# A decoder layer on one core: the second Sinkhorn group's products on GpSimd

## The chip, the core and the metric

The kernel runs on one core of a Trainium2 chip. The core has a matrix engine (TensorE, PE in the profile), a vector engine (VectorE, DVE), a scalar engine (ScalarE, ACT), GpSimd (POOL) and a queue engine (SyncE, SP) that here only issues transfers. Each engine works through its own list of instructions in a fixed order; between engines they wait for one another with semaphores. The metric is the time of one execution on the device in microseconds (us), lower is better; of several executions the median is taken.

## The reference

The input is 16 sequences of 128 tokens with 1024 features. Three layers are added to it one after the other: attention with rotary positions, an autocorrelation attention against a context, and a feed-forward layer that mixes four streams of 256 features. The change touches only the last one, and of it only the matrix that mixes the streams. Each token has a 4x4 matrix of logits, and 50 rounds of a Sinkhorn iteration turn it into one whose rows and columns sum to one:

```python
def step(carry, _):
    u, v = carry
    u = -logsumexp(Z + v[..., None, :], axis=-1)     # rows
    v = -logsumexp(Z + u[..., :, None], axis=-2)     # columns
    return ((u, v), None)
(u, v), _ = lax.scan(step, (u0, v0), None, length=50)
H_res = exp(Z + u[..., :, None] + v[..., None, :])
...
x_mixed = einsum('btij,btjc->btic', (1 - g) * I + g * H_res, x_streams)
```

## The kernel before

**The work as a whole.** The 128 tokens of a sequence lie on the 128 partitions. In a first stage (up to about 380 us) queries, keys, values and the spectra of the context are computed. Then 16 batches, one for each sequence, go through attention, autocorrelation, the logits of the streams (`logits`, L635 to L662) and the branch (`branch`, L664 to L712). Each batch is a Python generator; a heap with written-out waiting times (`T_...`, `PERIOD`, `SKS`) decides the order in which the generators record their work. A scheduler then places the recorded instructions in each engine's list, and so the lists of all engines can change where one instruction is moved.

**The Sinkhorn groups.** `ENDS = [7, 13, 16]` cuts the batches into three groups of seven, six and three. When the last batch of a group has its logits, `mixed` (L852) runs the iteration for all matrices of the group at once: one row of 128 partitions holds 7x16 = 112 numbers in the first group, 96 in the second, 48 in the third. Group 1's Sinkhorn therefore begins in mid-run and runs beside later batches; group 3's can only begin when batch 15, the last one, has its logits, and it is followed only by the closing work.

**The iteration.** `sinkhorn` (L719) makes the first round with logarithms, then seven blocks of seven rounds (`REFRESH = 7`). A block begins with the exponential `P` of the logits (L753 to L755) and ends with ACT's logarithm of the scale factors (L775) and their addition (L776); the last block ends with L778 and L779. A round has two halves, rows and columns. A half is a product `T` (L766 or L768), a sum of four (`s`, L770) and a reciprocal (`r`, L771), each needing the one before; the first half of a block has no product. So a group has 7 x 13 = 91 products, on an engine that a table picks:

```python
r = sk.tile([128, 2, n, 4], FP, name=f"r{gi % 2}", bufs=2)      # L759
for d in range(2):
    T = K
    if d or it:
        T = sk.tile([128, n, 4, 4], FP, name=f"T{gi % 2}", bufs=2)
        e = POOL if SKPS[gi] & (1 << d) else DVE                 # L764
        if d:
            e.tensor_mul(flat(T), flat(K), over(...r[:, 0]..., 4))   # L766
        else:
            e.tensor_mul(T, K, of_cols(ab[:, 1]))                # L768
    s = sk.tile([128, n, 4], FP, name=f"s{gi % 2}", bufs=2)
    DVE.tensor_reduce(s, turned(T) if d else T, AX.X, ALU.add)   # L770
    DVE.reciprocal(r[:, d], s)                                   # L771
```

`SKPS = [3, 0, 0, ...]` puts both halves' products of group 1 on GpSimd, and those of groups 2 and 3 on VectorE. Sums and reciprocals are on VectorE for all groups.

**What follows a group.** `mixed` scales the matrices (L858), lays them out for TensorE (`relaid`: L818 on DVE, L825 on PE, L829 on DVE), makes one token matrix for each batch (`token_matrix`, L833: on GpSimd for groups 1 and 2, on both engines for group 3) and multiplies (`mix`, L843 on PE). For groups 1 and 2 ACT copies the result (L885) and GpSimd issues a transfer that adds it to the output (L886); for group 3 VectorE adds it (L888) and SP or ACT issues the write (L889). GpSimd also computes two products for each cross-correlation (L574 and L575) and issues a transfer for each branch (L710).

Of the kernel before, what the change touches and what calls it, by code (L numbers as in the profile page):

```python
# [47 lines left out]
PRODS, T_PRE = [1,1,1], 15.0  # L48
T_FILL, T_SPEC = 37.36, 24.48
REUSE, LNA = 'tile', 11  # L50
SKPS = [3, 0, 0, 0, 0, 0]
BIG = 3.0e38
NEG = -1.0e30

# [58 lines left out]
def tile_decoder(ctx: ExitStack, tc, x, cx, wqkv, wo, wlog, base, gate, wb, mats, toks, zero, eye4, out):  # L113
# [605 lines left out]
    def sinkhorn(Z, n, gi):  # L719
# [32 lines left out]
        for block in range((ITERS - 1) // REFRESH):  # L752
# [5 lines left out]
            for it in range(REFRESH):  # L758
# [7 lines that stand above are left out]
# [245 lines left out]
```

## Time and profile before

| what | value |
|---|---|
| executions | 1218.52, 1213.81 and 1218.15 us, median 1218.15 |
| the profiled execution | 1218.14 us, span 1216.4 us, mean granted TensorE clock 0.932 |
| busy in the span | PE 1028.5, DVE 832.5, ACT 601.4, POOL 615.5 us |
| group 1's Sinkhorn | logits 739.0 (L856), closing product 1084.4 (L818) |
| group 2's Sinkhorn | logits 995.7, closing product 1166.3 |
| group 3's Sinkhorn | logits 1097.7, closing product 1200.1 |
| ACT's logarithms that end group 2's blocks (L775) | 1052.3, 1085.4, 1107.2, 1121.8, 1136.3, 1150.9 |
| the same of group 3's blocks | 1117.0, 1131.6, 1146.2, 1160.8, 1176.2, 1188.0 |

The times of the last rows are starts in us from the beginning of the span, read from the timeline. The span is that of the instructions; the execution's own time is 1.7 us longer. A busy share is a mean over stages that have different limits: TensorE is full for the first 1000 us and almost idle from 1108 on. What a change to a late stage is worth has to be read from that stage's own rows.

### The profile page before, as it was taken

What the parts mean: (1) busy time and instruction counts of PE and PEld (TensorE: products, weight loads), DVE (VectorE), ACT (ScalarE), POOL (GpSimd) and SP (SyncE); (2) the same over time, 40 slices, a digit from 0 to 9 for tenths busy, and PEclk for the clock granted to TensorE, in tenths of its full rate; (3) what the DMA queues carried; (4) which work ended last, traced back from release to release, by engine and by line L of the source; (5) the groups of instructions that cost most, each with busy time, mean ns of one, the idle gap of its engine ahead of it and who ended that gap; (6) DMA issues with size and microseconds to landing.
All of it is one profiled execution on the core that took longest, in us unless ns stands there. A gap on an engine that the chain in (4) does not pass through costs nothing.

```text
span 1216.4 us, 17264 instructions
## 1 busy us (share of the span) xinstructions
PE 1028.5 (85%) x5048; PEld 704.1 (58%) x5048; DVE 832.5 (68%) x2853; ACT 601.4 (49%) x1333; POOL 615.5 (51%) x655
## 2 busy tenths in 40 slices
PE   4999988989997989999999999899999987574043
PEld 2888756867874566566655665565556554243042
DVE  5454133223223478778877888898889989989986
ACT  3332222123332356676767767766776686553020
POOL 1444122313354256756685667667866876563040
PEclk9999999998997999999999999999999998788566
DMA  6764468277769247867776676666765647929135
GB/s 208 233 205 124 136 196 260 80 235 225 221 200 285 77 99 171 226 166 190 182 194 189 169 190 184 177 168 178 192 168 146 185 125 230 225 87 207 18 49 107
DMA packets 129246, 209.98 MB, mean 173 GB/s; under 512 B 12288, under 2 KB 76672, under 8 KB 129152
## 3 DMA queue, kind: packets, MB, share of 16 engines
q1 hardware_dynamic: 116416, 189.24, 55.0%
q0 software_dynamic: 9168, 15.21, 8.0%
q10 hardware_dynamic: 3568, 4.43, 1.2%
q8 instruction: 40, 0.66, 0.2%
q14 instruction: 54, 0.44, 0.1%
HBM read 130.78 MB, written 77.59 MB: 171 GB/s over the span
## 4 chain that ended last, share of the span: by engine, by line
PE 55%; DVE 23%; ACT 8%; DMA 7%; POOL 3%; issue 3%; SPq 1%; DVEq 0%; ACTq 0%; POOLq 0%
PE mm L341 5%; PE mm L342 5%; PE mm L343 5%; PE ps L564 5%; PE o L555 4%; PE o L556 3%; PE o L557 3%; DVE s L770 3%; DVE r L771 3%; PE ps L319 3%; PE sc L486 3%; DMA xt<-in_x 3%; PE sm L526 2%; PE sc L483 2%; ACT pt L516 2%
## 5 line engine op out<-in xcount | busy, mean ns | idle before, releaser
L574 POOL TENSOR_TENSOR s<-s,sv 128x512 f32<-128x512 f32 x96 | 123.6, 1290 | 55.4 <-ACT s L571 52.6
L575 POOL TENSOR_TENSOR P<-P,s 128x512 f32<-128x512 f32 x96 | 122.7, 1280 | 14.6 <-DVE P L573 12.0
L351 POOL TENSOR_TENSOR ra<-ra,rb 128x512 f32<-128x512 f32 x40 | 51.6, 1311 | 142.9 <-DVE rb L350 142.9
L555 PE MATMUL o<-pw,ch 128*128 128x512 f32 x256 | 108.0, 422 | 2.1 <-DVE xt L548 1.7
L517 POOL TENSOR_SCALAR_AFFINE_SELECT pt<-pt 128x512 f32<-128x512 f32 x128 | 83.9, 672 | 50.9 <-ACT pt L516 50.4
L556 PE MATMUL o<-pw,cl 128*128 128x512 f32 x256 | 105.0, 410 | 0.4 <-POOL cl L542 0.4
L557 PE MATMUL o<-pw,ch 128*128 128x512 f32 x256 | 101.1, 395 | 0.0
L486 PE MATMUL sc<-e,e 96*128 96x128 f32 x512 | 92.9, 310 | 0.8 <-DMA e<-qd 0.8
L493 DVE TENSOR_REDUCE mx<-sc 128x4 f32<-128x512 f32 x128 | 86.2, 677 | 7.8 <-PE sc L486 7.5
L486 PEld LDWEIGHTS sc<-e,e 96*128 96x128 f32 x512 | 78.0, 194 | 16.9 <-issue 12.5
L512 PE MATMUL sc<-e,e 98*128 98x512 f32 x128 | 65.8, 546 | 23.4 <-ACT pt L516 11.9
L573 DVE TENSOR_TENSOR P<-sv,ps 128x512 f32<-128x512 f32 x96 | 64.8, 675 | 24.7 <-ACT s L571 23.3
L320 ACT COPY F<-ps 128x512 f32<-128x512 f32 x64 | 35.9, 587 | 91.7 <-PE ps L319 45.2
L348 DVE TENSOR_TENSOR ra<-mm,am 128x512 f32<-128x512 f32 x40 | 26.1, 684 | 78.4 <-PE mm L343 64.8
L564 PE MATMUL ps<-wT,e 128*128 128x512 f32 x128 | 72.4, 656 | 7.5 <-DVE P L573 3.0
L771 DVE RECIPROCAL r<-s 128x28 f32<-128x28 f32 (+2 forms) x294 | 76.2, 272 | 2.5
L516 ACT ACTIVATE pt<-sc 128x512 f32<-128x512 f32 x128 | 72.7, 596 | 10.4 <-PE sc L512 8.6
L770 DVE TENSOR_REDUCE s<-T 128x28 f32<-128x112 f32 (+2 forms) x273 | 67.7, 260 | 14.6 <-POOL T L766 7.8
L319 PE MATMUL ps<-raw,am 128*128 128x512 f32 x128 | 67.8, 636 | 10.3 <-ACT F L320 10.0
L570 ACT COPY s<-ps 64x512 f32<-64x512 f32 x96 | 56.0, 583 | 38.2 <-PE ps L564 34.1
L825 PE MATMUL ps<-pt,spread 128*128 128x112 f32 (+2 forms) x24 | 5.7, 402 | 70.9 <-DVE s L770 52.2
L512 PEld LDWEIGHTS sc<-e,e 98*128 98x128 f32 x128 | 24.7, 200 | 61.9 <-ACT pt L516 30.7
(217 smaller groups left out, 2950.7 us busy)
## 6 DMA issues: line engine op xcount, KB each, us to landing
sv<-se SPq DMA_DIRECT2D x128, 256.0 KB
xt<-in_x SPq DMA_DIRECT2D x32, 512.0 KB
e<-qd SPq DMA_DIRECT2D x32, 512.0 KB
sv<-so SPq DMA_DIRECT2D x64, 256.0 KB
raw<-in_cx SPq DMA_DIRECT2D x16, 512.0 KB
so<-F SPq DMA_DIRECT2D x16, 512.0 KB
qd<-hi SPq DMA_DIRECT2D x32, 256.0 KB
qd<-lo SPq DMA_DIRECT2D x32, 256.0 KB
```

The source lines that it names most:

```text
L319: PE.matmul(ps, lhsT=A[m], rhs=cb[:, cols], start=True, stop=True)
L486: PE.matmul(sc[:, j, :], lhsT=qs[0:96, h * 128 : (h + 1) * 128], rhs=ks[0:96, g * 128 : (g + 1) * 128], start=False, stop=j == 3,)
L512: PE.matmul(st, lhsT=ks[:, g * 128 : (g + 1) * 128], rhs=qs[:, s * 512 : (s + 1) * 512], start=True, stop=True)
L516: ACT.activation(pt.rearrange("p j t -> p (j t)"), st, AF.Exp, scale=scale)
L555: PE.matmul(ps, lhsT=h, rhs=woh[k][:, cols], start=k == 0, stop=False)
L556: PE.matmul(ps, lhsT=r, rhs=woh[k][:, cols], start=False, stop=False)
L557: PE.matmul(ps, lhsT=h, rhs=wol[k][:, cols], start=False, stop=k == NK - 1)
L564: PE.matmul(ps, lhsT=M[m], rhs=of, start=True, stop=True)
L574: POOL.tensor_mul(s, s, v[:, 1, :])
L575: POOL.tensor_add(P, P, s)
L770: DVE.tensor_reduce(s, turned(T) if d else T, AX.X, ALU.add)
L771: DVE.reciprocal(r[:, d], s)
```

## The change

One entry of the table changes, and with it the engine of 91 instructions, the products L766 and L768 of group 2 with 128x96 numbers each. The arithmetic is the same.

```diff
-SKPS = [3, 0, 0, 0, 0, 0]
+SKPS = [3, 3, 0, 0, 0, 0]
```

Since the scheduler places all instructions anew, the order on VectorE and GpSimd also changes around the moved ones. Up to group 2's first product (at 1016 us in the profile) all the lists stand as they stood.

## The prediction

> **What bounds the kernel now.** I read the busy time by stretch first, because the page's shares are means over stages. Columns: stretch, then busy us and instruction count of PE, weight load, DVE, ACT and POOL, granted clock, DMA share, GB/s.
>
> ```profile
> 1015.00:1098.00 83.00, 54.07 (x206) 30.50 (x204) 77.84 (x325) 44.47 (x106) 50.10 (x59) 0.81 0.67 183
> 1098.00:1108.00 10.00, 5.02 (x16) 3.91 (x17) 9.32 (x53) 4.26 (x16) 0.39 (x1) 0.66 1.12 233
> 1108.00:1166.00 58.00, 6.73 (x32) 5.58 (x30) 57.35 (x352) 8.79 (x24) 6.91 (x6) 0.60 0.40 69
> 1166.00:1200.00 34.00, 14.71 (x56) 12.17 (x56) 28.33 (x124) 7.55 (x16) 13.69 (x12) 0.70 0.62 93
> 1200.00:1216.40 16.40, 9.85 (x32) 8.07 (x32) 6.89 (x11) 0.00 (x0) 1.54 (x1) 0.71 0.29 96
> ```
>
> All the moved products lie behind 1015 us. From there to 1166 us DVE is busy 94, 93 and 99% of the time, with groups 2 and 3 alone on it from 1108 on. So DVE looks like the bound. The timeline shows how they share it:
>
> ```profile
> 1143.21 0.26 DVE L768 TENSOR_TENSOR T<-P,r 128x96 f32<-128x96 f32 x1
> 1143.38 0.20 DVE L766 TENSOR_TENSOR T<-P,r 128x48 f32<-128x48 f32 x1
> 1143.50 0.39 DVE L770 TENSOR_REDUCE s<-T 128x24 f32<-128x96 f32 x2
> 1143.81 0.38 DVE L771 RECIPROCAL r<-s 128x24 f32<-128x24 f32 x2
> 1144.14 0.26 DVE L766 TENSOR_TENSOR T<-P,r 128x96 f32<-128x96 f32 x1
> ...
> 1145.13 0.26 DVE L768 TENSOR_TENSOR T<-P,r 128x96 f32<-128x96 f32 x1
> ...
> 1178.03 0.21 DVE L766 TENSOR_TENSOR T<-P,r 128x48 f32<-128x48 f32 x1
> 1178.27 0.23 DVE L770 TENSOR_REDUCE s<-T 128x12 f32<-128x48 f32 x1
> 1178.54 0.23 DVE L771 RECIPROCAL r<-s 128x12 f32<-128x12 f32 x1
> 1178.80 0.21 DVE L768 TENSOR_TENSOR T<-P,r 128x48 f32<-128x48 f32 x1
> ```
>
> Two halves of group 2 take 1145.13 - 1143.21 = 1.92 us, 0.96 each, and in that time group 3 makes a half too. Alone, a half of group 3 takes 1178.80 - 1178.03 = 0.77 us. So each chain fills the other's waits: group 2 costs group 3 only 0.19 us a half. By ACT's logarithms a block takes 14.55 us shared (1121.8 to 1136.3) and 11.8 us alone (1176.2 to 1188.0). These are latency chains rather than sums of work, and what counts is the round trip of a half.
>
> That round trip on POOL shows in group 1, where POOL and DVE happened to be free:
>
> ```profile
> 780.76 0.33 DVE L771 RECIPROCAL r<-s 128x28 f32<-128x28 f32 x1
> 781.24 0.39 POOL L768 TENSOR_TENSOR T<-P,r 128x112 f32<-128x112 f32 x1 [0.31 <-DVE r L771]
> 781.65 0.27 DVE L770 TENSOR_REDUCE s<-T 128x28 f32<-128x112 f32 x1 [0.57 <-POOL T L768]
> ```
>
> The reciprocal ends at 781.09 and POOL starts at 781.24: 0.15 us for the hand-over. The product takes 0.39, and DVE goes on 0.03 after its end.
>
> **The change part by part.** 91 products leave DVE (248 ns median) for POOL. Nothing else is added, but a DVE sum now waits for POOL, and every DVE instruction behind it in the list waits with it.
>
> *The product on POOL.* The trace has no 128x96 product there. It has 128x112 (median 384 ns) and 128x512 (L575, 1280 ns), so 896 ns for 400 numbers, 2.24 ns each: 384 - 16 x 2.24 = 348 ns. Bounds: 248 (as on DVE) and 384.
>
> *A half of group 2.* Sum, start to start of the reciprocal, 0.32 (0.25 or 0.32 long in turn, and 0.03 behind); reciprocal 0.30; hand-over 0.15; product 0.35; hand-back 0.03: 1.15 us. Group 3's three instructions take some 0.37 us of DVE in each such half, so either of group 2's meets one with a chance of a third and waits some 0.06: 0.03 more. I take 1.18 us, 0.22 more than before. Bounds 1.03 (product at 248 ns, hand-over as hidden as now) and 1.30 (a product of group 3, which also reads two buffers, meets POOL's). For that last case the row is
>
> ```profile
> 1094.02 1.31 POOL L833 TENSOR_TENSOR pt<-hs,e 128x512 f32<-128x512 f32 x1
> ...
> 1094.18 1.27 DVE L766 TENSOR_TENSOR T<-P,r 128x96 f32<-128x96 f32 x1
> ```
>
> where a 0.25 us product on DVE ends only 0.12 us behind POOL's. In the new list group 3's product often stands just ahead of group 2's sum, where POOL is at work.
>
> The Trainium skill, GPSIMD Engine Reference, section "Performance versus the Vector engine", speaks against the change: it has an elementwise two-input operation on GpSimd at 1.96 times VectorE's time, and names ordinary arithmetic as VectorE's work. The rows above give 1.4 times for this small size. By the page's ratio the product would be an estimated 486 ns, the half 0.14 us longer, and the 65 halves of five blocks 9 us longer, some 1231 us in the end; the row is nearer. Its section "Specifications" has the two engines share buffer interfaces when DVE reads two inputs, which the pair of rows at 1094 us agrees with.
>
> *A block of group 2.* 13 halves with a product, 15.3; the first half without, 0.75; from the last reciprocal over ACT's logarithm, three DVE steps and the exponential to the next sum, 1.6 (1107.0 to 1108.6): 17.7 us instead of 14.55.
>
> *Part 1, up to group 3's start (1097.7).* In the new lists 26 products (two blocks) lie ahead of it; the third block, of which half stood there, follows behind. What the 26 took on DVE, and how often DVE stood idle for group 1's products, as the model for the new wait (queries by source line and by tile):
>
> ```profile
> 1015.00:1086.00 71.00, 6.14 (x14) 4.64 (x11) 0.81 0.72 199
> 1015.00:1086.00 71.00, 5.49 (x12) 4.55 (x10) 0.81 0.72 199
> ...
>   POOL T L766: 7.8, 9
>   POOL T L768: 4.8, 6
> ```
>
> (L766 above, L768 below; the figures after the length are DVE's and POOL's.) Gone: 11.6 us. New waits: 12.6 us for 91, so 0.14 x 26 = 3.6. Group 1's 21 products on POOL in this stretch now each stand behind one of group 2's; waited out every time that is 21 x 0.35 = 7.4 us, and at POOL's busy share of 0.6 (50.1 of 83 us) 4.5. Sum: -11.6 + 3.6 + 4.5 = -3.5 us for group 1's end at 1084.4, and group 3's start follows that at the old distance. Before, the layout copy L829 (1086.9) to group 3's start took 10.8 us. In the new lists block 2's last two products stand on POOL behind six token products (L833, 6.1 us from 1087.3), one more (1.05) and a transfer (L886, 1.6), and DVE's row for batch 15's logits stands behind the reciprocal that needs them: 0.35 + 6.1 + 0.35 + 1.05 + 1.6 + 0.35 + 0.6 + 0.5 = 10.9. So nothing of that chain can be gained. Bounds: -11.6 (no wait at all) and +7 (rival A).
>
> *Part 2, from group 3's start to its last product.* Before: 1200.1 - 1097.7 = 102.4 us. In the new lists group 2 then still has five blocks, and group 3 ends block six just when group 2 ends. Five blocks are 88.5. In the first of these five, POOL also issues a branch's transfer and five of group 1's (0.9 and 5 x 1.3 = 7.4 us), each between two products; POOL's free 0.8 us of each half takes in 6 x 0.8 = 4.8 at best, but each issue waits for ACT first, so 4.4 of it stays (bounds 2.6 and 7.4). Then group 3's last block alone, 11.8, with group 2's closing steps between, 1.6. Sum 106.3: +3.9 us. So what group 3 gains per half it loses to the slower group 2, which runs beside it for longer: it was alone for 34 us and will be for 13.
>
> *Part 3, the end.* Group 2's closing work holds PE from its L818 (1166.3) to the last L843 (1183.2): 17 us. It had 34 us before group 3's came; now it has 13.4, and PE's list is in order. Group 3's L825 follows its L818 by 0.5, so it waits 17 - 13.4 - 0.5 = 3.1 us. GpSimd issues the last of group 2's six transfers near that time too, and group 3's last L833 stands behind them. Bounds 0 and 6.
>
> Costed at nothing: the 91 x 0.35 = 32 us of POOL, idle 33 of 83 us from 1015 to 1098 and 51 of 58 from 1108 on; ACT and the DMAs, which only follow; the 65 x 0.25 us that leave DVE behind 1098, since the chains and not DVE's work set the pace there.
>
> Sum: -3.5 + 3.9 + 3.1 = +3.5 us on the execution's own 1218.14 (span 1216.4), which stands at the median (1218.15): 1221.7, say 1222 us.
>
> **The rivals.**
> *A, slower: POOL's queue holds both chains before group 3's start.* Groups 1 and 2 alternate on POOL behind 1.28 us products (L574, L575) that wait for ACT and for transfers. For it: group 1's blocks, with products there, took 42 to 62 us (logarithms at 790.8, 852.3, 894.6, 945.6, 989.0, 1040.8). Against it: they ran beside more work, and POOL was still idle four tenths of 1015 to 1098. Group 2's first two blocks took 70.6 us together (1014.8 to 1085.4). From 81 us on group 3 starts no earlier than at present (2 us behind them) and the result is past 0.5%; at 44 us each it starts +7 (1014.8 + 88 + 2 against 1097.7) and the time is 1218.1 + 7 + 3.9 + 3.1 = 1232.
>
> *B, slower: the tail is more costly.* A half at 1.24 (product of group 3 caught behind POOL's) adds 65 x 0.06 = 4 us: 1226; at 1.30, 1229.5. It passes 0.5% from 1.22 us a half on.
>
> *C, faster: the round trip is hidden.* With a half at 0.96 as now, part 2 loses 65 x 0.22 = 14.3 us: 1207; at 1.03, 1212. It would need DVE's hand-overs to overlap with POOL's, which the rows at 781 us, where nothing else ran, speak against.
>
> **How the numbers follow.** 0.5% is 6.1 us, about what a measurement here tells from no change: 1212.1 to 1224.2. My forecast, a small loss within it, 0.47. A 0.22 and B 0.17 are slower; C 0.10 is faster, and 0.04 for small gains in part 1 that stay within. Same 0.51, slower 0.39, faster 0.10. The forecast's own range is 1216 to 1224. The range for 8 in 10 reaches to A's 1232 and a little past it, and to the upper end of C: 1211 to 1234.
>
> **What would show it.** Group 2's blocks in the tail at 17 to 18 us by ACT's logarithms (C: under 15.5; B: over 18.2); group 3 starting near 1094 (A: 1100 or later); group 2's L818 some 13 us ahead of group 3's, not 34; products on POOL near 0.35 us; PE's L825 of group 3 behind group 2's last L843. What would make it wrong is above all the place of the waits between 1016 and 1098, where both lists are full.

## The result and the profile after

The changed kernel takes 1226.00 us (median of 15 executions, 1221.06 to 1239.50). The kernel before, run in the same comparison, takes 1214.03 (15 executions, 1210.08 to 1220.21; the three shown earlier are its first). The ratio is 1.0089, with a 95% interval of 1.0070 to 1.0108: slower by some 10.8 us, and by more than the 0.5% that can be told from no change. One execution of the changed kernel (1239.50) ran in a slower state and is left out of the ratio but not of the median, and the two medians as they stand differ by 12.0 us.

The profiled execution of the changed kernel took 1223.47 us, with a span of 1221.7 and a mean granted clock of 0.927. That is only 5.3 us above the profile of before, but the two must not be compared from their beginnings. Group 2's logits, up to which the lists of both kernels are the same, come at 995.7 us in the profile before and at 991.3 after, and in the profiles of this study between 991.3 and 1004.4. So I count from there. Z (L856) is a group's scaled logits, with which its Sinkhorn begins. The four stretches are group 2's Z to group 3's Z, on to group 3's L818, on to the end of the last L888, and on to the end of the span:

| kernel | Z to Z | to L818 | to last L888 | to the end | sum | group 2's lead at L818 |
|---|---|---|---|---|---|---|
| before | 102.0 | 102.4 | 12.2 | 4.1 | 220.7 | 33.8 |
| changed | 101.4 | 106.4 | 11.4 | 11.2 | 230.4 | 13.4 |
| difference | -0.6 | +4.0 | -0.8 | +7.1 | +9.7 | |

The sum, +9.7 us, agrees with the 10.8 us of the timed executions. The -0.6 us of the first stretch lie within the spread: in four kernels further down that differ from the kernel before only behind group 3's Z, this stretch takes 100.7 to 102.6 us. The +4.0 of the second are clear of it (102.4 to 102.8 in three of the four). The largest term is in the last stretch, which is not a stretch of any engine's work.

Group 2's lead is the distance between the two groups' rows of L818, group 2's with 384 numbers on each partition and group 3's with 192. The first two rows are from before, the others from after:

```profile
1166.27 0.56 DVE L818 TENSOR_TENSOR pt<-P,e 128x384 f32<-128x384 f32 x1
1200.09 0.36 DVE L818 TENSOR_TENSOR pt<-P,e 128x192 f32<-128x192 f32 x1
...
1185.73 0.56 DVE L818 TENSOR_TENSOR pt<-P,e 128x384 f32<-128x384 f32 x1
1199.09 0.36 DVE L818 TENSOR_TENSOR pt<-P,e 128x192 f32<-128x192 f32 x1
```

The busy times by stretch of the changed kernel, with the columns of the table that opened the prediction:

```profile
1015.00:1098.00 83.00, 49.32 (x188) 27.08 (x187) 64.42 (x273) 43.42 (x106) 56.80 (x83) 0.77 0.75 196
1098.00:1108.00 10.00, 9.70 (x38) 8.29 (x39) 8.78 (x47) 6.27 (x15) 6.73 (x11) 0.83 0.65 128
1108.00:1166.00 58.00, 1.58 (x8) 1.05 (x6) 50.70 (x279) 5.08 (x17) 18.95 (x46) 0.53 0.30 52
1166.00:1200.00 34.00, 12.10 (x47) 10.40 (x48) 29.28 (x142) 6.38 (x15) 15.25 (x24) 0.59 0.12 16
1200.00:1221.70 21.70, 8.58 (x43) 7.22 (x41) 6.70 (x9) 2.10 (x4) 4.70 (x4) 0.82 1.00 193
```

DVE, which was busy 77.8 of the first 83 us, now works 64.4 and idles the rest, and group 3 starts no sooner for it. In the last row the DMA share is 1.00, where it was 0.29: the end belongs to transfers.

GpSimd's timeline in the tail, where a half of group 2 now runs (start, duration, engine, line, operation; in brackets the idle time before it and who ended it):

```profile
1143.09 0.35 POOL L768 TENSOR_TENSOR T<-P,r 128x96 f32<-128x96 f32 x1 [0.83 <-DVE s L770]
1144.21 0.40 POOL L766 TENSOR_TENSOR T<-P,r 128x96 f32<-128x96 f32 x1 [0.77 <-DVE r L771]
1145.46 0.40 POOL L768 TENSOR_TENSOR T<-P,r 128x96 f32<-128x96 f32 x1 [0.85 <-DVE r L771]
1146.63 0.35 POOL L766 TENSOR_TENSOR T<-P,r 128x96 f32<-128x96 f32 x1 [0.77 <-DVE T L766]
```

The products take 0.35 to 0.40 us here, and a half takes 1.12, 1.25 and 1.17 us, start to start: 1.18 on average. Group 2's blocks, by ACT's logarithms at 1115.2, 1132.7, 1150.1 and 1167.6, take 17.4 to 17.5 us.

Now the last stretch, in rows of the same kind. Before:

```profile
1200.00:1203.00 3.00, 1.91 (x8) 1.78 (x8) 0.77 (x4) 0.00 (x0) 0.09 (x1) 0.50 0.00 0
1203.00:1212.00 9.00, 7.94 (x24) 6.29 (x24) 5.81 (x8) 0.00 (x0) 1.45 (x1) 0.68 0.22 75
1212.00:1216.40 4.40, 0.00 (x0) 0.00 (x0) 0.31 (x1) 0.00 (x0) 0.00 (x0) 0.91 0.61 205
```

and after:

```profile
1200.00:1203.00 3.00, 3.00 (x19) 2.74 (x17) 0.00 (x0) 2.10 (x4) 2.25 (x2) 1.00 1.17 173
1203.00:1212.00 9.00, 5.58 (x26) 4.48 (x25) 6.70 (x9) 0.00 (x0) 2.45 (x3) 1.00 1.23 194
1212.00:1221.70 9.70, 0.00 (x0) 0.00 (x0) 0.00 (x0) 0.00 (x0) 0.00 (x0) 0.60 0.73 199
```

The last two columns are the DMA share and GB/s. Before, the transfer engines have nothing to do from 1200 to 1203, and after that only group 3's three writes. After, they are full from 1200 to 1212, at 173 and 194 GB/s, and move another 199 GB/s behind 1212, where no compute engine works any more. The clock, the column before these two, is 0.50 and 0.68 before and 1.00 after, and the same 24 matmul instructions of group 3 (L843) take 7.94 us before and 5.42 after. Both facts are taken up below.

### The profile page after: what moved, and what is told of

Its sections match the earlier page's. It is cut to its first block, busy times and chain, and to the rows that moved or that the text cites. A ratio compares the mean times of both kernels' runs of the same rounds, so it can differ in the third digit from the quotient of the medians.

```text
span 1221.7 us, 17342 instructions
## 1 busy us (share of the span) xinstructions
PE 1022.9 (84%) x5048; PEld 701.5 (57%) x5048; DVE 816.8 (67%) x2762; ACT 602.2 (49%) x1333; POOL 646.8 (53%) x746
## 4 chain that ended last, share of the span: by engine, by line
PE 54%; DVE 19%; ACT 9%; DMA 7%; POOL 5%; issue 4%; SPq 1%; DVEq 0%; POOLq 0%; ACTq 0%
PE mm L341 5%; PE mm L343 5%; PE mm L342 5%; PE ps L564 5%; PE o L555 3%; PE o L556 3%; PE o L557 3%; DVE s L770 3%; PE ps L319 3%; PE sc L486 3%; DMA xt<-in_x 3%; DVE r L771 3%; PE sm L526 2%; ACT pt L516 2%; PE sc L483 2%
## 5 line engine op out<-in xcount | busy, mean ns | idle before, releaser
L557 PE MATMUL o<-pw,ch 128*128 128x512 f32 x256 | 101.0, 395 | 0.0
L486 PEld LDWEIGHTS sc<-e,e 96*128 96x128 f32 x512 | 77.6, 193 | 17.1 <-issue 12.2
L770 DVE TENSOR_REDUCE s<-T 128x12 f32<-128x48 f32 (+2 forms) x273 | 69.2, 261 | 27.1 <-POOL T L766 16.6
L512 PE MATMUL sc<-e,e 98*128 98x512 f32 x128 | 67.1, 557 | 22.9 <-ACT pt L516 12.2
L825 PE MATMUL ps<-pt,spread 128*128 128x112 f32 (+2 forms) x24 | 4.9, 364 | 78.7 <-DVE s L770 76.8
L766 POOL TENSOR_TENSOR T<-P,r 128x96 f32<-128x96 f32 (+1 forms) x98 | 39.5, 404 | 55.3 <-DVE r L771 28.7
```

What stands on the lines that cost most here:

```text
L486: PE.matmul(sc[:, j, :], lhsT=qs[0:96, h * 128 : (h + 1) * 128], rhs=ks[0:96, g * 128 : (g + 1) * 128], start=False, stop=j == 3,)
L557: PE.matmul(ps, lhsT=h, rhs=wol[k][:, cols], start=False, stop=k == NK - 1)
```

## The experiments

My theories after reading the two profiles were three, one for each stretch. *End:* group 2 closes 13.4 us ahead of group 3 instead of 33.8, so that its six accumulating transfers (L886) run into group 3's writes. *Tail:* the round trip of a half, as predicted. *Start:* something other than DVE's work holds group 3's Z. The rivals were that GpSimd's queue ahead of group 3's Z makes the loss (rival A of the prediction), and that the round trip makes all of it. The kernels of this section give these stretches; the ratio is to the kernel before, run on the same chip:

| kernel | ratio, 95% | Z to Z | to L818 | to last L888 | to the end | sum | lead |
|---|---|---|---|---|---|---|---|
| plain writes, changed kernel | 1.0039 (1.0009 to 1.0068) | 101.0 | 106.9 | 11.5 | 4.4 | 223.8 | 13.4 |
| plain writes, kernel before | 1.0019 (0.9997 to 1.0040) | 100.7 | 102.4 | 12.5 | 4.1 | 219.8 | 33.8 |
| first two blocks on GpSimd | 1.0034 (1.0011 to 1.0057) | 101.6 | 104.0 | 11.3 | 4.1 | 221.0 | 28.8 |
| last five blocks | 1.0046 (1.0021 to 1.0071) | 100.8 | 107.8 | 10.5 | 7.0 | 226.2 | 17.9 |
| L766 alone | 1.0101 (1.0073 to 1.0130) | 103.9 | 111.5 | 12.3 | 4.1 | 231.9 | 32.1 |
| no products for group 2 | 1.0047 (1.0022 to 1.0073) | 110.8 | 99.1 | 11.7 | 4.1 | 225.6 | 87.4 |
| first block on GpSimd | 1.0076 (1.0052 to 1.0100) | 111.3 | 102.8 | 12.5 | 4.1 | 230.7 | 35.4 |
| group 1's token matrix once | 1.0006 (0.9981 to 1.0031) | 101.6 | 106.5 | 11.6 | 4.7 | 224.3 | 18.7 |
| group 1's last block on DVE | 1.0092 (1.0063 to 1.0122) | 108.4 | 107.2 | 11.6 | 4.3 | 231.5 | 18.7 |
| 25 idle matmuls | 1.0014 (0.9985 to 1.0042) | 102.6 | 104.0 | 12.2 | 4.1 | 223.0 | 35.4 |
| 15 idle matmuls | 0.9981 (0.9954 to 1.0008) | 102.3 | 102.7 | 8.9 | 4.1 | 218.0 | 34.1 |
| 12 idle matmuls | 1.0003 (0.9986 to 1.0020) | 102.5 | 102.8 | 11.4 | 4.1 | 220.8 | 34.2 |

"Plain writes, kernel before" differs from the kernel before only in its last 50 us, and yet its median came out 0.2% higher, while its profile shows the same stretches within 1.3 us. So differences of 0.2 to 0.3% between medians are not read here, and the stretches carry the argument.

### The end: are the transfers the cause?

```diff
-POOL.dma_start(out=tokens_on(out[b]), in_=z, accum_op=ALU.add)
+if gi == 1:
+    POOL.dma_start(out=tokens_on(out[b]), in_=z)
+else:
+    POOL.dma_start(out=tokens_on(out[b]), in_=z, accum_op=ALU.add)
```

In the changed kernel:

> The changed kernel with group 2's six output transfers (L886 for group 2) made plain writes from the same GpSimd queue in place of accumulating ones; the output rows of batches 7 to 12 then lack what was accumulated earlier. Theory 'the end is held by group 2's transfers': in the profile after, six accumulating transfers of 512 KB run from about 1197.5 at 190 to 200 GB/s, 16 us, and group 3's three plain ones at about 345 GB/s, 4.5 us, can only finish behind them, near 1218. Plain, the six need about 9 us at 345 GB/s and are over before group 3's, so the time from the last L888 to the end falls from 11.2 us to 4 to 6 us: 5 to 7 us less than the changed kernel, a ratio to the kernel before of 1.002 to 1.005. Rival 'the round trip of the half alone makes the loss': nothing changes, 1.007 to 1.011.

and in the kernel before:

> The same plain writes in the kernel before (same part of the output left out). Theory 'the end is held by group 2's transfers': there they end near 1194, 20 us before the end, so nothing changes: 0.999 to 1.001. Rival 'accumulating transfers slow whatever runs beside them': 3 us or more less, 0.9975 or below.

The queue's row and the issues' row from 1180 us on in the changed kernel (packets, MB, share of the engines; count, KB each, median us from issue to landing):

```profile
q0 software_dynamic: 3168, 3.15, 46.4%
...
out<-pw POOLq DMA_DIRECT2D x6, 512.0 KB, 9.9
```

and with plain writes, from 1190 on:

```profile
q0 software_dynamic: 864, 3.15, 35.3%
...
out<-pw POOLq DMA_DIRECT2D x6, 512.0 KB, 3.6
```

The same 3.15 MB go in 864 packets instead of 3168, and a transfer lands in 3.6 us instead of 9.9. The stretch from the last L888 to the end falls from 11.2 to 4.4 us, a loss of 6.8, with all else in place (101.0, 106.9, 11.5). The ratio falls from 1.0089 to 1.0039, which is the 5 to 7 us that were expected. In the kernel before nothing is gained: 4.1 us both times. So the transfers make 6 to 7 us of the loss, and only because they come late.

How late is too late shows in the lead column. With accumulating transfers and a lead of 28 us and more the last stretch is 4.1 us; at 18.7 us it is 4.3 and 4.7, at 17.9 it is 7.0 and at 13.4 it is 11.2. Counted from group 2's L818 instead, the end comes 34.6, 34.9, 35.4 and 36.0 us behind in these four kernels, nearly the same each time, as it should where group 2's transfers set the end and not group 3. The rates give an estimate of the lead that they need. The changed kernel issues the first L886 9.1 us behind group 2's L818 (1194.8 against 1185.7):

```profile
1194.81 1.26 POOL L886 DMA_DIRECT2D out<-pw  x1
...
1201.80 2.71 POOL L886 DMA_DIRECT2D out<-pw  x2 [0.75 <-ACT pw L885]
```

Six transfers at 194 GB/s take 3.15 / 0.194 = 16.2 us, so with 1.3 us for the first issue they would be through some 27 us behind group 2's L818. Group 3's first write (L889) is issued 8.3 us behind its own L818. The difference is 18 to 19 us. It is a low estimate: in the kernel before, where nothing else moved, the last of the six landed 29.8 us behind group 2's L818 (1196.1 against 1166.3), which would make the lead 21 to 22 us.

### The tail and the start: the change by halves

```diff
-e = POOL if SKPS[gi] & (1 << d) else DVE
+e = POOL if SKPS[gi] & (1 << d) and (gi != 1 or block < 2) else DVE
```

> Group 2's products on GpSimd in its first two blocks only (26 of 91), which end near group 3's start; on DVE after that. Theory 'the loss is made behind group 3's start, by the round trip of a half (block of 17.5 for 14.6 us) and the late closing that follows from it': tail and end as before, so only part 1 is left. By the prediction's part 1 that is -3.5 us (0.997), by the trace after -0.5 us (0.9996): 0.996 to 1.001. Rival 'GpSimd's queue ahead of group 3's start makes the loss' (rival A): 1.004 to 1.010.

and with `block >= 2`:

> The other part alone: group 2's products on GpSimd in blocks 3 to 7 only (65 of 91), on DVE before. Theory 'the loss is made behind group 3's start': nearly all of it is there, +4 us by group 3's slower blocks and +6 to 7 us by the late closing, 1.007 to 1.011. Rival A (queue ahead of group 3's start): 1.003 or less.

The last five blocks alone give +5.5 in the sum of stretches (107.8 instead of 102.4 in the second, 7.0 instead of 4.1 in the last, and 1.2 and 1.7 us less in the other two) and 1.0046. That is less than I expected, because the lead is 17.9 us and not 13.4: group 2 has its first two blocks on DVE there and enters the tail earlier. The first two blocks alone show no gain at all in the first stretch (101.6), so the -3.5 us that the prediction put there do not exist; their sum is +0.3. Their median, 1.0034, is higher than my range and than that sum; where the rest lies isn't shown by the profile, whose own execution took 1222.41 us with group 2's Z as late as 999.3. Rival A would need a later Z of group 3 in this kernel, and it isn't there.

Together the halves give 5.8 us, the whole 9.7. The sum is not linear, since the lead falls from 33.8 to 28.8 by the one and to 17.9 by the other: the first two blocks delay group 2 (its second logarithm comes 101.4 us behind its Z, and 89.7 before), the others slow it, and only both together push the transfers well into the end.

### Half of the products in every round

```diff
-SKPS = [3, 3, 0, 0, 0, 0]
+SKPS = [3, 2, 0, 0, 0, 0]
```

> Only the products of L766 of group 2 on GpSimd (49 of 91), those of L768 on DVE. Theory 'round trip plus late closing': the round trip costs in proportion, +2 us from group 3's Z to its L818 (104 to 105 us); group 2's lead over group 3 at L818, 33.8 us before and 13.4 after, becomes 22 to 26, which is more than the 20 us from which the six transfers (over some 28 us behind L818) reach into group 3's closing (its first write 8 us behind L818), so the end stays at 15.5 to 16.7 us behind L818: ratio 1.000 to 1.003. Rival 'half the products, half the loss': 1.0045, with the end 19 us behind L818.

Both expectations failed: with 49 products moved, the loss is as large as with 91 (1.0101). The lead stays at 32.1 and the end at 4.1, as it does wherever the lead is so long, but the second stretch takes 111.5 us, 5 more than with all products moved. DVE's timeline in that tail:

```profile
1144.64 0.32 DVE L770 TENSOR_REDUCE s<-T 128x24 f32<-128x96 f32 x1 [0.21 <-POOL T L766]
1144.87 0.20 DVE L766 TENSOR_TENSOR T<-P,r 128x48 f32<-128x48 f32 x1
...
1146.75 0.32 DVE L770 TENSOR_REDUCE s<-T 128x24 f32<-128x96 f32 x1 [0.21 <-POOL T L766]
1146.98 0.20 DVE L766 TENSOR_TENSOR T<-P,r 128x48 f32<-128x48 f32 x1
```

In DVE's list the two groups alternate here, two halves of group 2 against two of group 3, so group 3's product stands behind group 2's waiting sum each time. Both take 2.11 us for two halves, and both groups' blocks take some 16.0 us (logarithms at 1131.6, 1147.5, 1163.6 and at 1138.2, 1154.0, 1170.1). With all products on GpSimd the list is a different one: group 2 takes 17.5 us a block, and group 3 keeps its 14.5. From 1115 to 1165 us VectorE waits for GpSimd's products 20 times with half of them moved (5.0 us) and 13 times with all (3.4 us). So what the waits cost did not follow the number of moved products; these two lists show it go by what stands behind each wait.

### What holds group 3's start

Four kernels ask why 13.4 us less DVE work between 1015 and 1098 bring group 3's Z nothing.

```diff
-if d or it:
+if (d or it) and gi != 1:
```

> The kernel before with group 2's 91 products left out altogether (its sums read K itself; the mixing of batches 7 to 12 is then wrong): the most that taking them off DVE could bring, with no GpSimd in it. From group 2's Z (L856) to group 3's Z is 102.0 us in the profile before and 101.4 after, though DVE's work there fell from 96.8 to 83.2 us. Theory 'GpSimd's queue and the waits on it ate that gain': without the products and without GpSimd the 13 us come, 88 to 92 us. Rival 'DVE is the bound only in the first half of that stretch; behind it the last batch's own chain (transfers, ACT, GpSimd) and group 1's chain set the pace': 97 to 100 us. In the tail, from group 3's Z to its L818, 102.4 before and 106.4 after: half an iteration of group 2 loses 0.35 us of DVE, so 85 to 95 us. Ratio 0.980 to 0.990.

With the test from the change by halves at `block < 1`:

> Group 2's products on GpSimd in its first block only (13 of 91), on DVE after that. With two blocks there, the stretch from group 2's Z to group 1's sixth log fell from 45.1 to 41.6 us, and the next one, group 1's last block, rose from 43.6 to 47.0. Theory 'both chains on GpSimd lengthen group 1's last block': with group 2 back on DVE from its second block the first gain stays and the loss does not come, group 3's Z 97 to 99 us behind group 2's Z, 3 us less, ratio 0.996 to 0.999. Rival 'group 3's Z is set by the last batch's own chain, whatever group 1 does': 100.5 to 102, ratio 0.999 to 1.002.

And group 1's token matrix made once:

```diff
-hm = q3.tile([128, 4, 32, 4], FP, name="pt", bufs=NB["pt"])
-token_matrix(hm, hs, t, POOL)
+if gi != 0 or t == 0:
+    hm = q3.tile([128, 4, 32, 4], FP, name="pt", bufs=NB["pt"])
+    token_matrix(hm, hs, t, POOL)
```

> The changed kernel with group 1's token matrix (L833) built once instead of seven times, so that GpSimd's burst behind group 1's L829 is gone; batches 1 to 6 then use batch 0's weights. From group 1's L818 to group 3's Z: 13.0 us in the changed kernel, 13.3 before. Theory of the prediction's part 1, 'products of group 2 behind the six L833 hold DVE ahead of group 3's Z' (waits of 2.96 and 2.01 us): 8 to 10 us. Rival 'TensorE's order holds it': L825, the first L833, then 8 L843, L650, 8 L843, L656 and L660 stand one behind the other there in both kernels (L660 ends 0.6 us before L661 after, 1.1 us before), and group 1's L829 comes 91.21 us behind group 2's Z in both: 12 to 13 us. The ratio follows within the measurement: 1.004 to 1.009.

And group 1's last block back on DVE (`gi != 0 or block < 6` in that test):

> The changed kernel with group 1's products of its last block back on DVE. From group 1's sixth log to its L818: 46.9 us in the changed kernel, 43.6 before. Theory 'two chains on GpSimd lengthen group 1's last block': 40 to 44 us, group 3's Z 97 to 99 us behind group 2's Z. Rival 'the batches' own chain (transfers, ACT, GpSimd) paces that block through DVE's fixed order': 45 us or more, group 3's Z at 100.5 or more, whichever engine has the products. Behind group 3's Z nothing changes: 128 to 130 us to the end.

Both ranges for the kernel without products were wrong: 110.8 us, with neither products nor GpSimd, and 99.1 us in the tail instead of 85 to 95. Its ratio is 1.0047, so even without group 2's products this schedule is no faster. The kernel is not the clean limit that I took it for. A sum that reads K itself no longer waits for the reciprocal before it, so that group 2's halves are not a chain any more; the lists fill the freed time with later halves of group 2, which closes 87.4 us ahead of group 3, and DVE is busy for 102.8 of the 110.8 us. For one block on GpSimd both ranges were wrong too: group 3's Z came 111.3 us behind group 2's, and group 1's last block took 49.9 us although group 2 was back on DVE. What came no sooner in any of these is the batches' own work. Batches 13, 14 and 15 write their outputs (L637) 19.7, 59.2 and 88.0 us behind group 2's Z in the kernel before, and 19.7, 58.0 and 87.3 in the changed one. In all fourteen profiles, with and without group 2's products, the last of the three lies between 86.7 and 91.2 us. So freed DVE time did not bring batch 15 forward in any of them. What is left is that its own chain of transfers, ACT, GpSimd and TensorE sets its pace, beside which DVE had its gaps filled with Sinkhorn halves. No run changes that chain, so this is argued and not shown, and which link of it is the tight one wasn't settled.

From group 1's closing on, the rows point to TensorE's order as what holds group 3's Z. TensorE's timeline in the changed kernel:

```profile
1083.95 3.78 PE L843 MATMUL ps<-mz,pt 128*128 128x256 f32 x8 [1.49 <-POOL pt L833]
1087.52 1.15 PE L650 MATMUL ps<-ident,z 128*128 128x128 f32 x8
1088.51 1.95 PE L843 MATMUL ps<-mz,pt 128*128 128x256 f32 x8
1090.39 0.64 PE L656 MATMUL ps<-zT,e 128*32 128x128 f32 x16
1091.42 0.40 PE L660 MATMUL ps<-e 128*128 128x24 f32 x2 [0.39 <-ACT e L657]
```

and with one token matrix for group 1, where GpSimd's burst is gone:

```profile
1086.01 3.67 PE L843 MATMUL ps<-mz,pt 128*128 128x256 f32 x8 [1.49 <-POOL pt L833]
1089.52 1.04 PE L650 MATMUL ps<-ident,z 128*128 128x128 f32 x8
1090.39 1.97 PE L843 MATMUL ps<-mz,pt 128*128 128x256 f32 x8
1092.29 0.65 PE L656 MATMUL ps<-zT,e 128*32 128x128 f32 x16
1093.32 0.40 PE L660 MATMUL ps<-e 128*128 128x24 f32 x2 [0.39 <-ACT e L657]
```

The chain is the same to 0.2 us, although DVE waits only 0.30 and 1.24 us for GpSimd there instead of 2.96 and 2.01; from group 1's L818 to group 3's Z it takes 12.5 us instead of 13.0. So the waits that the prediction counted on that path lie beside it. That TensorE's order is what holds it is read from the rows, which follow one another almost without a gap; no run changes that order. What the burst does hold is group 2: with the burst gone its next logarithm comes 95.9 us behind its Z instead of 101.3, the lead grows to 18.7 us, the last stretch falls to 4.7 us and the ratio to 1.0006 (the sum of its stretches, 3.6 us above that of before, would be 1.003). My expectation of 1.004 to 1.009 was wrong in that. It is the second way in which the loss at the end goes when the lead comes back.

Group 1's last block did take 43.7 us with its products on DVE, as the theory wanted, instead of 46.9. Behind group 3's Z it took 123.1 us to the end and not the 128 to 130 expected, because group 2's lead is 18.7 us there and the last stretch 4.3: a third way. But group 3's Z was 108.4 behind group 2's, because another thing came in its place, which the kernel with one block on GpSimd shows as well. DVE's row there:

```profile
1090.62 7.49 DVE L753 TENSOR_TENSOR P<-Z,uv 128x96 f32<-128x96 f32 x1
```

beside GpSimd's:

```profile
1090.02 0.89 POOL L710 DMA_DIRECT2D out<-mx  x1 [5.14 <-ACT prod L775]
1090.68 7.30 POOL L833 TENSOR_TENSOR pt<-hs,e 128x512 f32<-128x512 f32 x7
```

A subtraction that takes 0.26 us elsewhere lasted until all seven token products were through, and batch 15's rows stood behind it. With group 1's last block on DVE the same line took 6.98 us, and without products a product of group 3 took 5.95 us in the burst of group 2's L833. In the first two of these kernels it lies on the way to group 3's Z, and Z to Z takes 111.3 and 108.4 us; in the third it lies in group 3's own first block.

### TensorE's clock in the closing

```diff
+if gi == len(ENDS) - 1 and block == (ITERS - 1) // REFRESH - 1 and it >= 2:
+    if it == 2:
+        idle = ps_f.tile([128, 256], FP, name="ps", padded_shape=[128, 512])
+    PE.matmul(idle[:, 0 : 4 * n], lhsT=ident, rhs=r[:, 0].rearrange("p t i -> p (t i)"), start=True, stop=True)
+    for k in range(4):
+        PE.matmul(idle, lhsT=ident, rhs=wb_sb[:, k % 2, :], start=True, stop=True)
```

> The kernel before with 25 idle matmuls on TensorE beside group 3's last block (results unused). In the profile before TensorE stands idle for 17 us ahead of group 3's closing, its clock is 0.50 to 0.68 there, and the 8 matmuls of L825 and 24 of L843 take 1.91 and 7.94 us; in the profile after, behind group 2's matmuls and at a clock of 1.00, the same take 1.01 and 5.42 us. Theory 'that clock is why group 3's closing from L818 to the last L888 got no longer in the changed kernel in spite of the wait for TensorE': with the idle matmuls the 12.2 us become 8.5 to 9.5 and the time falls by 2.5 to 3.5 us, ratio 0.997 to 0.998. Rival 'the closing is bound by DVE's adds and the writes': 1.000, or 1.001 by the matmuls that stand ahead of L825.

With `it in (1, 2, 3, 4, 5)` and two wide ones each:

> The kernel before with fewer idle matmuls beside group 3's last block than in the first such run: two of 128x256 and a small one behind each of iterations 2 to 6 (iteration 7 has none). In that first run L825 and group 3's 24 L843 took 1.01 and 5.42 us, as in the changed kernel, but the idle ones stood ahead of L825 until 4.7 us behind L818 (hs L829 5.06 us behind L818, 2.52 in the kernel before), so L818 to the last L888 stayed at 12.2 us. Theory 'TensorE's clock holds the closing': with the idle ones gone before L818, hs comes 1.6 us behind L818 and the last L888 8.5 to 9.5 us behind it, 2.7 to 3.7 us less: ratio 0.997 to 0.998, a version below both kernels. Rival 'the clock falls back in the gap, or DVE's adds and token matrices hold the closing': 11 us or more, ratio 0.999 to 1.001.

With `it in (0, 1, 2, 3, 4, 5)` and one each:

> The same with one idle matmul of 128x256 and a small one behind each of iterations 1 to 6: TensorE is then busy for about half of the time only. Theory 'any recent work keeps the clock': as with two, 8.5 to 9.5 us from L818 to the last L888. Rival 'the clock answers to how densely TensorE is busy': L825 and L843 stay near 1.9 and 7.9 us, 11.5 to 12.5 us from L818 to the last L888, ratio 1.000.

TensorE's timeline in the closing of the kernel before:

```profile
1200.60 1.91 PE L825 MATMUL ps<-pt,spread 128*128 128x48 f32 x8 [17.37 <-DVE pt L818]
1203.65 7.94 PE L843 MATMUL ps<-pw,pt 128*128 128x256 f32 x24 [1.14 <-issue]
```

and with 15 idle matmuls, where L778, L831 and L849 are the wide idle ones, L825 and L843:

```profile
1193.17 2.05 PE L778 MATMUL ps<-e,ident 128*128 128x256 f32 x4
...
1199.57 1.14 PE L778 MATMUL ps<-e,ident 128*128 128x256 f32 x4
...
1202.33 1.08 PE L831 MATMUL ps<-pt,spread 128*128 128x48 f32 x8 [0.54 <-DVE pt L824]
1204.55 5.42 PE L849 MATMUL ps<-pw,pt 128*128 128x256 f32 x24 [1.14 <-issue]
```

With 12 (L825 and L843 again, under the same line numbers):

```profile
1199.14 1.92 PE L831 MATMUL ps<-pt,spread 128*128 128x48 f32 x8 [1.74 <-DVE pt L824]
1202.20 7.15 PE L849 MATMUL ps<-pw,pt 128*128 128x256 f32 x24 [1.14 <-issue]
```

So the clock is what the closing hangs on: 15 idle matmuls take it from 12.2 to 8.9 us. 25 brought the same short rows but stood ahead of L825 themselves and made the stretch before longer by 1.6 us (104.0), and nothing was left of the 3 us (12.2). 12 did not bring the clock up ahead of L825; it rose only 3.5 us into L843 (11.4). My expectation called TensorE busy for half of the time there, which the stretch beside them doesn't show:

```profile
1188.00:1197.00 9.00, 9.00 (x24) 5.52 (x24) 7.50 (x35) 0.00 (x0) 0.00 (x0) 0.50 0.64 102
```

By its first column TensorE is busy for all of the 9 us, and the clock stays at 0.50. What is less is what it worked through: twelve matmul instructions of 256 columns and twelve small ones in 9 us, where with 15 idle matmuls twelve of 256 columns and eight small ones took 6.8 us, and then the clock rose. A busy PE in the profile is not a dense one. That the density decides fits these two runs and isn't shown beyond them. This is why the changed kernel's closing got no longer in spite of the wait for TensorE: group 2's matmuls stood directly ahead of group 3's, and gave back in clock (7.94 to 5.42 us, and 1.91 to 1.01) what their place in the queue cost. The version with 15 has the lowest sum of all, 218.0 us, and a median of 1214.62 against 1216.27, a ratio of 0.9981. Its interval, 0.9954 to 1.0008, still reaches to no change.

## Why the prediction was right or wrong

The predicted 1222 us is 4 us below the measured median, and the range held it. That it came so near is partly luck: the forecast started from 1218.15 us, and the kernel before came out at 1214.03. As a difference it was +3.5 us where the executions show 10.8. The likeliest case, a small loss within 0.5%, did not come; the loss is beyond it, by a way that none of the rivals names.

- **The half and the block of group 2: right.** 1.18 us predicted and measured, 17.7 and 17.4 to 17.5; the product from the slope between two sizes was 348 ns, the rows show 345 to 400. (The 248 ns on DVE that it was held against is a median over both sizes of L768; the 128x96 products alone have 258, so the ratio is 1.35 and not 1.4.) So neither rival B (1.22 and more) nor C (1.03 and less) came.
- **Part 2: right, by its terms too.** 106.3 us predicted, 106.4 measured. From group 3's Z to group 2's L818 it is 93.0 us, where five blocks and the late issues made 92.9; the first of the five, with the issues in it, took 22.6 us (22.1 predicted).
- **Part 1: wrong.** -3.5 us became -0.6. The step that failed is "-11.6 + 3.6 + 4.5 = -3.5 us for group 1's end": it read 94% busy as the bound. Group 1's L829 comes 91.2 us behind group 2's Z in both profiles, and batch 15's output 88.0 and 87.3 us. The profile has group 3's Z at 1092.7, which looks like the 1094 that the prediction asked for, but its group 2 also began 4.4 us sooner. The stretch behind L829 was sized right (10.9 predicted, 10.2 measured), but for the wrong reason: the waits for GpSimd lie beside it, and the rows point to TensorE's order.
- **Part 3: the wait came, its cost did not.** The lead of 13.4 us was right to the tenth. Group 3's L825 began 3.1 us behind L818 instead of 0.5, a wait of 2.6 us where 3.1 was predicted, but took 1.01 us instead of 1.91, so that the layout copy L829 came only 1.7 us later. The stretch to the last L888 even got 0.8 us shorter, because TensorE was at full clock.
- **The step that made the result: "ACT and the DMAs, which only follow", costed at nothing.** The prediction saw that the lead falls to 13.4 us and named the late issues of GpSimd in a sentence, but priced the lead for TensorE alone. For the transfers it had to be 18 us or more, and the end lost 7.1 us; with plain writes in their place 6.8 of them came back.
- **Rival A: wrong.** Group 3's start was not late.

The net of parts 1 to 3 was +3.5 predicted and +2.6 measured (-0.6 + 4.0 - 0.8). What lay between a small loss and the measured one was the transfers.

## What to carry to other kernels

When a change delays one of two streams that finish one behind the other, write down how far ahead the first one finishes, and hold that lead against everything that closes it: its matmuls, its issues, and the time that its transfers need on engines shared with the last writes. An engine that is 94% busy over a stretch is the bound only if the milestones of that stretch move with its work, so look for a milestone (a batch's output) before counting freed time as gained. And where lists are placed anew, ask what the list puts behind each wait: half of this change cost as much as the whole.

## What the runs showed of the hardware

- **The clock of TensorE in a short closing.** After 17 us without matmuls, L825 and the first half of group 3's L843 ran at half rate (granted clock 0.50). From the first matmul of a row until the granted clock rose to 1.00 it took 3.5 us (L843 in the kernel with 12 idle matmuls), 5.2 (L843 before), 6.0 (25 idle matmuls) and 6.9 (15). With twelve passes of 256 columns in 9 us it did not rise at all, though the profile shows TensorE as busy throughout. The Trainium skill, TensorE: Matmul & The Clock Gate, Part 1, has the array at half rate by default and at full rate after a busy window of about 3.4 us, a window that runs freely and does not begin with the first matmul. The two rates agree with these rows, and no time here is shorter than that window; what makes a window a busy one the rows leave open.
- **GpSimd's bursts can hold a VectorE instruction with two buffer inputs for their whole length**: 7.49 us behind seven products, 6.98 and 5.95 behind six. The Trainium skill, SBUF — State Buffer, section "Who interferes with whom", says that a VectorE instruction with two inputs from the buffer contends with a GpSimd instruction that reads it. For how long it says only for VectorE's two-port modes (the whole of one instruction); here it was up to seven. In the kernel before, products that met a burst of six took 1.06 and 0.86 us. The fourteen profiles hold 27 bursts of six or seven: in the three long cases a transfer issue of GpSimd overlapped the burst's start, in the other 24 none did, and there no such VectorE instruction took more than 1.11 us. That the issue decides was not tried.
- **Accumulating transfers** of 512 KB landed in 9.9 us and plain ones from the same queue in 3.6 us, each the median of six that follow one another; their packets were 1 KB and 3.6 KB on average.
